# A four-layer convolution network on one core: the first function of each group of gelus or silus gets the lowest priority

## The chip, the cores and the metric

The kernel runs on one core of a Trainium2 chip. The metric is the device time of one execution in microseconds, the median of several runs. "ScalarE" is called ACT in the profile, "VectorE" DVE, "GpSimd" POOL, "TensorE" PE, and "SyncE", which issues most DMAs, SP.

## The reference, cut to what matters

Four layers follow each other on an input of 4 images of 64 x 64 tokens with 128 channels:

```python
x = _L0_conv_ref(x, ...)   # layernorm, projection, 3x3 depthwise conv, silu, selective scan in 4
                           # directions, layernorm, gate, projection, layernorm, MLP with gelu
x = _L1_conv_ref(x, ...)   # attention over all 4096 tokens
x = _L2_conv_ref(x, ...)   # 1x1 and 3x3 convolutions with hard_swish
x = _L3_conv_ref(x, ...)   # neighbourhood attention over 7 x 7, layernorm, MLP with gelu
```

The core of layer 0 is a recurrence over the 4096 tokens, for each of 256 channels and 16 states:

```python
def step(h, t):
    x_t, d_t, B_t, C_t = t
    h = jnp.exp(d_t[..., None] * A) * h + (d_t * x_t)[..., None] * B_t[:, :, None, :]
    return (h, jnp.einsum('bkdn,bkn->bkd', h, C_t))
```

## The kernel before, in words

The four images pass through the same stages. `scan_inputs` makes what the recurrence reads (delta, delta times x, B and C rows) and puts it into DRAM. `selective_scan` runs the recurrence of one image. `rest` does everything else for an image: `scan_output` (gate, projection and MLP of layer 0, and beside it, by turns, `layer3_mlp` of the image before), `layer1`, `layer2` and `layer3_attention`. `network` records scan(0), the scan inputs of the images 1 to 3, and then scan(i) followed by rest(i - 1). The last rest, of image 3, runs after the last scan with wider tiles.

In the scan a pair of 32 channels with 4 states fills 128 partitions, and time is cut into chunks of 512 steps. A unit of it is: GpSimd multiplies `du` by a B row (L501, 128 x 1024); ScalarE makes two "decays", exp(delta x A), of 128 x 512 each in PSUM (L507, three buffers); VectorE runs the recurrence over each (L509); the product with the C row is made by VectorE (L514) or, for 7 of 16 units (5 in image 0), by GpSimd (L522); ScalarE copies the last column as the state for the next chunk (L516 for one, L518 for two); TensorE sums over the states (L555). An image has 1024 decays, all four have 4096.

The exponential and the logarithm share one table set of ScalarE, which is the one that stays loaded. Gelu and silu need other sets. So they are done in groups: the class `Together` collects the functions of a group, lets all of them wait for the group's last matmul, and has the exponential's set loaded again behind them by `exp_table` (L96). There are 100 groups: 36 of up to four silus in `scan_inputs` (L359, L376), and 64 of four gelus in `mlp` (L226) and in the wide form of layer 3 (L1301). A group of gelus is then followed by the second product of its MLP (L233), which waits for it.

The order of each engine's instructions is fixed when the program is built. A scheduler goes through a simulated time and gives an engine, of the instructions that are ready, the one with the lowest priority number. Recorded code gets growing numbers from zero; `priority(tc, K, base)` gives what stands inside it numbers from `base` on. The scan has the base SCAN_FIRST = 10,000,000, so all else goes before it where both are ready. The groups have -100 x SCAN_FIRST: as soon as they are ready they go before everything. Which buffers are free is part of "ready".

Layernorm (L174 to L202) is mostly on ScalarE: two functions for the deviation, one for the sign (L192), four shifts (L194), four normalisations (L198), and one copy with scale and bias behind the transposition (L202).

Of the kernel before, what the change touches and what calls it, by code (L numbers as in the profile page):

```python
# [54 lines left out]
BEHIND = 2  # L55
ON_POOL = ((1, 4, 7, 10, 13), (0, 2, 4, 6, 9, 11, 13))
SCAN_FIRST = 10_000_000

# [16 lines left out]
@contextmanager  # L77
def priority(tc, K, base):

    kept = tc.cur_priority  # L80
    tc.cur_priority = K.next_priority.get(base, base)
    yield
    K.next_priority[base] = tc.cur_priority
    tc.cur_priority = kept


def after(tc, later, earlier, kind=mybir.DependencyClass.Sync):
    tc.add_manual_dep(
        later.ins, earlier.ins.name, mybir.DependencyInfo(kind, mybir.DependencyReason.DATA), reason="group"
    )  # L90


def exp_table(tc, K, done):

    with priority(tc, K, -100 * SCAN_FIRST):
        load = tc.nc.scalar.preload_act_table_set("natural_log_exp_and_others")  # L96
        after(tc, load, done, mybir.DependencyClass.NoSync)


class Together:  # L100
# [8 lines left out]
            after(self.tc, matmul, self.done)  # L109

    def run(self, last_matmul, acts):
        with priority(self.tc, self.K, -100 * SCAN_FIRST):
            for act in acts:
                self.done = act()
                after(self.tc, self.done, last_matmul)
        exp_table(self.tc, self.K, self.done)


# [146 lines left out]
def make_conv_diagonals(tc, K, A, out):  # L265
    nc = tc.nc
    with tc.tile_pool(name="mk_conv", bufs=1) as pool:
        convw = pool.tile([128, ND, 9], F32, name="convw")
        nc.sync.dma_start(convw, A["L0_conv_conv_w"])
        diag = pool.tile([128, ND, 9, 128], F32, name="conv_diag")  # L270
        for d in range(ND):
            for t in range(9):
                nc.scalar.activation(diag[:, d, t, :], K.ident, AF.Copy, scale=convw[:, d, t : t + 1])
        nc.sync.dma_start(out, diag)
# [1423 lines left out]
def network(tc, A, out):  # L1698
    nc = tc.nc
    with ExitStack() as ctx:  # L1700
# [26 lines left out]
        with ExitStack() as scan_ctx:  # L1727
            S = make_scan(scan_ctx, tc, K, A)
            make_conv_diagonals(tc, K, A, D.conv_diag)
            with priority(tc, K, SCAN_FIRST // 2):  # L1730
                with tc.tile_pool(name="mk_w2", bufs=1, side="right") as pool:
# [3 lines left out]
            for img in range(B):  # L1735
                with priority(tc, K, SCAN_FIRST):
                    selective_scan(tc, K, S, D, img)
# [94 lines left out]
```

## Time and profile before

| | |
|---|---|
| median of 3 runs | 8846.92 us (8845.23 to 8850.76) |
| the profiled execution | 8838.78 us, span 8837.0 us |
| busy: PE, DVE, ACT, POOL | 7047.0, 7137.4, 5686.9, 7046.7 us |
| decays (L507) | 4096, 690 ns each, 2781.9 us |
| B products (L501) | 2048, 2375 ns each, 4805.9 us |
| C products on GpSimd (L522) | 832, 2376 ns each, 1976.6 us |
| gelus (L226) | 224, 688 ns each, 135.5 us |
| loads of the gelu's table (L226) | 56, 1283 ns each, 71.8 us |
| loads of the exponential's table (L96) | 100, 1283 ns each, 128.3 us |

A row of a group in the profile gives line, engine, operation and tile, the count, the busy time, the mean of one and the idle time of its engine just before, with what ended it. A row of the timeline gives the start, the duration, and the idle time before it in square brackets. In a row of stretches of the span each engine's busy time stands with its count, then the granted clock of TensorE, the DMA engines' busy share and GB/s.

### The profile page before, as it was taken

How to read it: one execution, taken by the hardware profiler on the slowest of the kernel's cores; microseconds unless marked ns; L12 is line 12 of the kernel's file. 1: busy time of each engine (PE TensorE's matmuls, PEld its weight loads, DVE VectorE, ACT ScalarE, POOL GpSimd, SP SyncE). 2: the span in 40 equal slices, each digit the busy share in tenths (PEclk: the TensorE clock that was granted, in tenths of full speed). 3: DMA queues.
4: the chain of work that ended last, by engine and by line, in shares of the span. 5: the costliest groups of instructions: out<-in, count | busy, mean ns of one | idle time of the engine just before them, and what ended most of it. 6: DMA issues, size and time to landing. Idle time of an engine off the chain costs nothing. (4 is left out here: it accounts for less than half of the span.)

```text
span 8837.0 us, 102218 instructions
## 1 busy us (share of the span) xinstructions
PE 7047.0 (80%) x30532; PEld 2635.0 (30%) x30532; DVE 7137.4 (81%) x8531; ACT 5686.9 (64%) x11661; POOL 7046.7 (80%) x3079
## 2 busy tenths in 40 slices
PE   6745858687788898786788988877789887788988
PEld 2211313132332222333322223333322223344333
DVE  4788978787999999998899999998899999513433
ACT  5646767676676676666766676667766666454366
POOL 6888998989899999997799999998899989500000
PEclk8756869697799998898899998888899998899989
DMA  5777777777554556665455556575455565320020
GB/s 185 244 232 247 241 251 240 260 242 262 189 170 165 170 170 219 191 211 190 160 168 173 174 174 227 194 224 176 156 171 174 176 217 192 108 70 5 1 82 12
DMA packets 855474, 1572.03 MB, mean 178 GB/s; under 512 B 218341, under 2 KB 336764, under 8 KB 851197
## 3 DMA queue, kind: packets, MB, share of 16 engines
q1 hardware_dynamic: 724605, 1389.21, 48.1%
q10 hardware_dynamic: 130304, 176.19, 5.6%
q8 instruction: 245, 4.01, 0.2%
q14 instruction: 320, 2.62, 0.1%
HBM read 1273.92 MB, written 280.18 MB: 176 GB/s over the span
## 5 line engine op out<-in xcount | busy, mean ns | idle before, releaser
L501 POOL TENSOR_TENSOR dB<-du,b_rows 128x1024 f32<-128x1024 f32 x2048 | 4805.9, 2375 | 477.2 <-issue 124.7
L507 ACT ACTIVATE dA<-dt,w_A_log 128x512 f32<-128x512 f32 x4096 | 2781.9, 690 | 510.8 <-DVE hc L509 246.7
L509 DVE TENSOR_TENSOR_SCAN dA<-dA,state,dB 128x512 f32<-128x512 f32 x2128 | 2631.5, 1272 | 275.6 <-POOL dB L501 131.8
L522 POOL TENSOR_TENSOR hc<-hc,c_rows 128x1024 f32<-128x1024 f32 x832 | 1976.6, 2376 | 47.0 <-ACT state L518 21.7
L509 DVE TENSOR_TENSOR_SCAN hc<-dA,state,dB 128x512 f32<-128x512 f32 x1456 | 1801.1, 1267 | 180.5 <-ACT dA L507 105.8
L514 DVE TENSOR_TENSOR hc<-dA,c_rows 128x512 f32<-128x512 f32 x2432 | 1564.5, 675 | 74.4 <-PE py L555 59.3
L555 PE MATMUL py<-hc,pick 128*32 128x512 f32 x8192 | 1245.1, 683 | 392.0 <-POOL hc L522 299.8
L516 ACT COPY state<-dA 128x1 f32<-128x1 f32 x2128 | 326.9, 158 | 1271.7 <-DVE hc L514 1260.1
L845 PE MATMUL pa<-e,l_v 128*128 128x512 f32 x2048 | 1062.5, 651 | 20.3 <-ACT e L801 20.3
L797 PE MATMUL pair<-l_g,l_f 32*128 32x512 f32 x2048 | 532.8, 667 | 165.7 <-ACT e L801 119.1
L801 ACT ACTIVATE e<-pair 128x1024 f32<-128x1024 f32 (+1 forms) x448 | 508.4, 1135 | 231.4 <-PE pair L797 222.8
L985 POOL MEMSET l_h<- 64x128 f32 x8 | 1.6, 197 | 814.9 <-DVE l_h L959 814.9
L845 PEld LDWEIGHTS pa<-e,l_v 128*128 128x128 f32 x2048 | 374.3, 199 | 670.9 <-issue 615.1
L555 PEld LDWEIGHTS py<-hc,pick 128*32 128x32 f32 x8192 | 210.1, 116 | 1161.4 <-issue 471.1
L247 PE MATMUL ps<-band,w_conv_diag 128*128 128x504 f32 (+3 forms) x1152 | 500.4, 594 | 6.0 <-ACT delta L397 6.0
L1351 PE MATMUL pair<-table,ident 128*128 128x512 f32 x768 | 408.2, 657 | 98.7 <-ACT e L1361 76.2
L509 DVE TENSOR_TENSOR_SCAN dA<-dA,dB 128x512 f32<-128x512 f32 x304 | 356.1, 1212 | 66.3 <-POOL dB L501 52.5
L201 PE MATMUL ps<-ident,ln_xn 128*128 128x128 f32 x512 | 141.9, 371 | 325.2 <-ACT ln_xn L198 253.2
L328 POOL TENSOR_TENSOR du<-delta,xc 128x1024 f32<-128x1024 f32 x128 | 333.3, 2611 | 52.6 <-ACT delta L397 46.7
L1361 ACT ACTIVATE e<-pair 128x1024 f32<-128x1024 f32 (+1 forms) x224 | 254.8, 1137 | 178.6 <-PE pair L1355 177.8
L247 PEld LDWEIGHTS ps<-band,w_conv_diag 128*128 128x128 f32 x1152 | 221.3, 193 | 283.9 <-issue 263.8
L797 PEld LDWEIGHTS pair<-l_g,l_f 32*128 32x128 f32 x2048 | 140.6, 189 | 523.9 <-ACT e L801 264.4
(285 smaller groups left out, 8746.8 us busy)
## 6 DMA issues: line engine op xcount, KB each, us to landing
b_rows<-bc_dram SPq DMA_DIRECT2D x1024, 256.0 KB
c_rows<-bc_dram SPq DMA_DIRECT2D x1024, 256.0 KB
dt<-delta_dram SPq DMA_DIRECT2D x512, 512.0 KB
du<-du_dram SPq DMA_DIRECT2D x512, 512.0 KB
delta_dram<-delta ACTq DMA_DIRECT2D x128, 512.0 KB
du_dram<-du SPq DMA_DIRECT2D x128, 512.0 KB
table<-biasT_dram SPq DMA_DIRECT2D x72, 512.0 KB
y_first_dram<-y_sum ACTq DMA_DIRECT2D x128, 256.0 KB
```

Of the source, the lines that this page charges most:

```text
L247: mm = nc.tensor.matmul(out[:, r0 - row0 : r1 - row0, c0:c1], lhsT((dy + 1) * 3 + dx + 1), src[:, r0 + dy : r1 + dy, c0 + dx : c1 + dx], s ...
L328: nc.gpsimd.tensor_mul(du.rearrange("p d (a b) -> p d a b", b=H), deltas[b].rearrange("p d (a b) -> p d a b", b=H), tk,)
L501: nc.gpsimd.tensor_mul(dB, dus[pp], mid(bt, 2))
L507: nc.scalar.activation(dA, dts[pp][:, g, :], AF.Exp, scale=S.A[:, k, j, pr, g : g + 1])
L509: nc.vector.tensor_tensor_scan(hg[:, order], dA[:, order], dB[:, g, order], 0.0 if i == 0 else state[:, j, pr, g : g + 1], ALU.mult, ALU.add,)
L514: mm = nc.vector.tensor_mul(hc[:, g, :], dA, ct)
L522: made.append(nc.gpsimd.tensor_mul(hc, hc, mid(ct, 2)))
L555: mm = nc.tensor.matmul(py[0][32 * q : 32 * q + 32, :], S.pick, hcs[q // 2][:, q % 2, :], start=(k == 1 and j == 0), stop=(j == NJS - 1),)
L797: nc.tensor.matmul(ps[:, u, :], f[quad, t // 4, span(t % 4, 128)], g[quad, c, :], start=True, stop=True)
L801: made = nc.scalar.activation(e, ps, AF.Exp)
L845: nc.tensor.matmul(pa, v[:, 8 * q + t, :], es[q], start=(t == 0 and q == 0), stop=(t == 7 and q == 3),)
L1351: nc.tensor.matmul(ps[:, u, :], K.ident, t[:, u, :], start=True, stop=False)
```

## The change

In `Together.run` the first function of a group gets the base LAST x SCAN_FIRST = 500,000,000 in place of -100 x SCAN_FIRST, so that on its engine every other instruction that is ready goes before it. The others keep their number, and an order without a semaphore (NoSync) is added that puts them behind the first. The load of the exponential's set keeps its number and its place behind the last function.

```diff
 SCAN_FIRST = 10_000_000
+LAST = 50
...
     def run(self, last_matmul, acts):
-        with priority(self.tc, self.K, -100 * SCAN_FIRST):
-            for act in acts:
+        first = None
+        for act in acts:
+            with priority(self.tc, self.K, (LAST if first is None else -100) * SCAN_FIRST):
                 self.done = act()
                 after(self.tc, self.done, last_matmul)
+            if first is None:
+                first = self.done
+            else:
+                after(self.tc, self.done, first, mybir.DependencyClass.NoSync)
         exp_table(self.tc, self.K, self.done)
```

No computation is changed. What it changes is the built order of each engine's instructions. Behind the change, the line numbers of the kernel are 6 higher.

## The prediction

> **What bounds the kernel now.** I read the page first: VectorE (DVE) 81% and GpSimd (POOL) 80% busy, ScalarE (ACT) 64%, TensorE (PE) 80%. That is an average over stages, so I cut the span at the points where the sources of line change: scores of layer 1 (L801), attention products of layer 3 (L1384, L1390), scan_output (L618, L656). Busy time by stretch of the span, the stretch in front:
>
> ```profile
> core 0: us, PE busy (x) PEld busy (x) DVE busy (x) ACT busy (x) POOL busy (x), PEclk, DMA share, GB/s
> 4003.00:4453.00 450.00, 340.77 (x1378) 171.09 (x1378) 371.07 (x526) 325.02 (x736) 357.35 (x155) 0.83 0.53 172
> 4460.00:5130.00 670.00, 607.51 (x2472) 181.32 (x2470) 633.23 (x673) 445.61 (x844) 665.25 (x288) 0.94 0.53 172
> 5910.00:6358.00 448.00, 344.43 (x1379) 174.31 (x1379) 383.41 (x539) 327.62 (x724) 371.31 (x160) 0.83 0.55 179
> 6360.00:7030.00 670.00, 609.79 (x2505) 184.05 (x2502) 635.34 (x673) 452.21 (x876) 665.84 (x288) 0.95 0.52 172
> 7300.00:7600.00 300.00, 241.75 (x1397) 92.92 (x1390) 282.62 (x313) 194.50 (x417) 299.90 (x131) 0.86 0.58 192
> 7640.00:7770.00 130.00, 104.55 (x661) 44.64 (x660) 3.90 (x12) 33.41 (x45) 0.00 (x0) 0.93 0.14 42
> ```
>
> In layer 1 and layer 3 under a scan POOL is busy 99% and more: the scan runs at POOL's pace. In the two stretches that hold scan_output and the MLP of the image before (450 and 448 us, called A and B below) POOL is at 79% and 83%, and nothing is full: there engines wait for each other. The last row has no scan left at all, and layer 3 of image 2 still runs. VectorE's timeline at that place:
>
> ```profile
> 7636.64 1.27 DVE L514 TENSOR_TENSOR hc<-dA,c_rows 128x512 f32<-128x512 f32 x2
> 7672.43 0.69 DVE L1384 TENSOR_TENSOR oT<-rec,po 128x512 f32<-128x512 f32 x1 [34.52 <-ACT rec L1382]
> ...
> 7772.99 0.69 DVE L1390 TENSOR_TENSOR x<-x,pj 128x512 f32<-128x512 f32 x1 [2.17 <-PE pj L1388]
> 7776.04 0.27 DVE L600 MEMSET center<- 128x256 f32 x1 [2.36 <-DMA x_dram<-x]
> ```
>
> The last scan ends at 7638, layer 3 of image 2 at 7774, and only then does the final stage (L600, then 1061 us to the end) begin. The other hand-overs look alike: layer 3 of image 1 ends at 5896 and L618 of image 2 starts at 5910. So the end is set by the chain of rest() calls, one after the other, not by the scan alone.
>
> What ties the two: ACT's list is one fixed sequence in which rest's functions stand between decays (L507). Taking times of the 4096 decays from the trace, layer 1 passes 402 and 403 decays in 667.0 and 666.5 us, 1.657 us each, which is POOL's pace. A passes 210 decays in 445.0 us and B 216 in 441.7, so A is 97 us and B 84 us over that pace. Why, shows a gelu group on ACT (timeline) and then on DVE:
>
> ```profile
> 4094.01 0.14 ACT L516 COPY state<-dA 128x1 f32<-128x1 f32 x1
> 4094.16 1.28 ACT L226 ACT_TABLE_LOAD   x1
> 4095.46 2.42 ACT L226 ACTIVATE mlp_h<-ps,w_fc_b 128x512 f32<-128x512 f32 x4
> 4097.90 1.28 ACT L96 ACT_TABLE_LOAD   x1
> 4099.19 0.16 ACT L516 COPY state<-dA 128x1 f32<-128x1 f32 x1
> 4099.25 0.70 ACT L507 ACTIVATE dA<-dt,w_A_log 128x512 f32<-128x512 f32 x1
> ```
> ```profile
> 4094.48 1.27 DVE L514 TENSOR_TENSOR hc<-dA,c_rows 128x512 f32<-128x512 f32 x2
> 4099.98 1.29 DVE L509 TENSOR_TENSOR_SCAN dA<-dA,state,dB 128x512 f32<-128x512 f32 x1 [4.23 <-ACT dA L507]
> ```
>
> 5.02 us without a decay, and VectorE idles 4.23 us for one. Adding up VectorE's idle time from each group's start to 1.5 us after its end gives 52 us over the 16 groups of A and 48 over the 16 of B, 3.1 us a group.
>
> **What the Trainium skill says.** "ScalarE: Activation LUTs", section "What ACT_TABLE_LOAD costs", gives 1283 ns for a load plus some 1380 ns of drain. The trace agrees on 1283 (16 loads, mean 1283 ns) and not on the drain: the gelu starts 0.02 us after the load, and two loads and four gelus make 5.02 us. "TensorE: Matmul & The Clock Gate", section "Architectural detail", says that ACT's and DVE's queues are strictly first in, first out; the rows above agree, the ready decay stands behind the group. "Perfetto Trace Analysis", section "Optimization Strategy", asks to look for gaps inside the regime concerned; hence A and B alone.
>
> **The change part by part.** No instruction is added or removed, and the two loads per group stay, so direct work is 0. What moves is decided when the program is built, and I compared the two built orders.
>
> 1. Where it acts. ACT's order is the same up to position 6155 of 12239, which is 4036 us in the trace, and again from 7802 us on. The 36 silu groups and the first 8 gelu groups already stood behind the decays; the last 24 have no scan beside them. Only 32 gelu groups, those of A and B, move. Cost outside: 0, since those sequences are identical.
>
> 2. Decays before the group. Counting decays minus state copies ahead of each group gives the decays ready in the three PSUM buffers: 2.75 on average in A before and 2.9 after, 2.4 and 2.3 in B. So they mostly stood there already; what now moves ahead of gelus is as much layernorm work (L194, L198) as decays.
>
> 3. Length of the stretches without a decay. I add ACT's work between each two decays from the rows' means (load 1.283, gelu 0.605, L198 0.42, L194 0.21, state 0.15 to 0.19 us) and take what exceeds 3.9 us, two decays' work of VectorE (twice 1.27 for L509 and 0.675 for L514). A: 46.8 us before, 37.1 after. B: 36.6 before, 39.0 after. Price: A and B differ by 13.2 us over the pace and by 10.2 in this sum, 1.3 us for each. So A gains 9.7 x 1.3 = 12.6 us and B loses 2.4 x 1.3 = 3.1: together -9.5 us. From below: all groups as long as now, 0; from above: all VectorE idle time in the groups gone, -100.
>
> 4. The lead of rest over the scan. Counting decays that stand before the same step of rest: the first score function of layer 1 has 2271 before it in both orders for image 1, and 3347 before, 3333 after for image 2. The lead shrinks to 3 at the start of layer 3 and is 16 again at L1381 of the fifth chunk, 4077 against 4061. Those 16 decays no longer stand between rest and its end; at the trace's 1.65 us each (204 decays from number 3857 to 4061 took 337.1 us) it is -26.5 us. Afterwards 16 more decays run beside the last three chunks: the sixth took 68.7 us partly under the scan, a full one takes some 79, so I give 3 us back. Can rest go that fast? Image 1's first chunks of layer 3 held 46, 45 and 45 decays and took 74.2, 73.7 and 72.2 us; later ones held 50, 49 and 51 and took 86.1, 82.9 and 85.7. Image 2 goes from 48 a chunk to 45, a rate already seen.
>
> 5. Other queues. DVE, PE and SP follow the same plan; POOL's list differs in 59 of 3083 places. SP's loads of x (L612, L1330) move up by as much as 14 places, among transfers that use half the DMA engines' time; I cost them at nothing, one missed landing would be some 2.4 us, as the L188 wait for x in A.
>
> Sum: -9.5 - 26.5 + 3 = -33 us. Against the profiled execution (8838.78, span 8837.0, 1.8 around it) that is 8806; it lies 8 us under the median, so for the median I say 8846.9 - 33 = 8814.
>
> **The rivals.** (a) TensorE paces layer 3, not the decays: PE is 80% busy there with and without scan, and its busy time counts waits badly. Then the lead is worth nothing, as the products (L555) it passes only come later, and -9.5 us remain: 8837. The 45-decay chunks speak against it. (b) The gelus become late. A group that waits for one more layernorm block waits 4 x 0.21 + 4 x 0.42 = 2.5 us; the 16 groups of scan_output lie on rest's chain (the other 16, of the image before, have slack): +40 us, 8887. It decides if the fc2 products behind the gelu, not the shared list, set when a chunk ends; the gain of 33 is lost from 2.1 us a group on. For it: gelus now follow L194 and L198 blocks in several groups. Against: rest's steps stand at equal or smaller decay counts at the end of A and B. (c) Stalls fall further: seven of the first eight gelu groups, which have always stood behind a decay, leave VectorE idle 1.8 us each. If all 32 come down to that, 32 x 1.3 = -42, with the lead -65: 8782. Against: step 2.
>
> **How the numbers follow.** Forecast 0.58, (a) 0.20, (b) 0.10, (c) 0.12. Some 0.2% (18 us) is what a measurement of this kernel can tell from no change. Of the forecast 0.52 lies beyond it; with (c) and a little of (a), faster 0.67; the rest of (a) and of the forecast, same 0.22; (b), slower 0.11. The range 8782 to 8853 ends at (c) below and takes in all of (a) above; beyond it lie (b) and part of (c). The forecast's own range is 8795 to 8830.
>
> **What would show it.** Right: A shorter by some 12 us with POOL above 80% in it; B with 10 decays fewer; layer 3 of image 2 ends near 7741 instead of 7774, and some 115 us instead of 136 after the last scan. Step 3 is wrong if A is as long as before; step 4 if five chunks of layer 3 take as long with 45 decays each as with 48. Wrong altogether: gelus that hold up L233, seen as PE idle time released by mlp_h growing, or a final stage of other than 1061 us.

## The result, and the profile after

The changed kernel takes 8832.41 us (median; 8822.39 to 8842.44), the kernel before, run beside it, 8849.52 us. The ratio is 0.9981, 95% interval 0.9975 to 0.9987: 17 us faster (12 to 22), where 33 were forecast. Its profiled execution took 8831.36 us, 7.4 less than that of before; but up to decay 2061, where both run the same order, it had already lost 7.7 us (its B products took 2388 ns each up to there, against 2370). From there to the end it is 15.1 us shorter, which agrees with the medians.

The same stretches as before the change, cut at the same sources of line (busy time by stretch of the span, kernel after):

```profile
core 0: us, PE busy (x) PEld busy (x) DVE busy (x) ACT busy (x) POOL busy (x), PEclk, DMA share, GB/s
4011.00:4451.00 440.00, 342.48 (x1372) 169.85 (x1373) 370.76 (x526) 324.56 (x736) 356.93 (x155) 0.84 0.55 176
5908.00:6346.00 438.00, 336.35 (x1375) 162.42 (x1373) 370.79 (x525) 320.69 (x706) 352.03 (x152) 0.85 0.54 175
6350.00:7020.00 670.00, 605.60 (x2447) 181.40 (x2446) 635.39 (x675) 449.14 (x872) 666.82 (x289) 0.94 0.52 172
7300.00:7600.00 300.00, 245.62 (x1416) 94.14 (x1408) 280.63 (x312) 194.94 (x418) 299.71 (x131) 0.86 0.60 193
7650.00:7760.00 110.00, 87.78 (x528) 37.75 (x528) 3.91 (x12) 27.20 (x38) 0.00 (x0) 0.89 0.15 50
```

A (first row) holds the same 526 VectorE and 155 GpSimd instructions as before, in some 10 us less. B (second row) is shorter too, but with 152 GpSimd instructions in place of 160: 206 decays fall into it, not 216. In layer 3 of image 2 (fourth row) TensorE does 1416 products in 300 us where it did 1397, with no more VectorE work: rest goes faster there, and fewer decays stand in its way (counted below). The last row, without a scan, is what the change shortened most. VectorE's timeline at the scan's end, kernel after:

```profile
7646.01 1.27 DVE L520 TENSOR_TENSOR hc<-dA,c_rows 128x512 f32<-128x512 f32 x2
...
7764.20 0.69 DVE L1396 TENSOR_TENSOR x<-x,pj 128x512 f32<-128x512 f32 x1 [1.51 <-PE pj L1394]
7767.25 0.27 DVE L606 MEMSET center<- 128x256 f32 x1 [2.36 <-DMA x_dram<-x]
```

From the last scan product to the final stage it was 7637 to 7776; now it is 7646 to 7767. A gelu group of A on ACT, kernel after:

```profile
4093.80 0.69 ACT L513 ACTIVATE dA<-dt,w_A_log 128x512 f32<-128x512 f32 x1 [1.10 <-DVE hc L515]
4094.51 1.28 ACT L232 ACT_TABLE_LOAD   x1
4095.80 2.42 ACT L232 ACTIVATE mlp_h<-ps,w_fc_b 128x512 f32<-128x512 f32 x4
4098.24 1.28 ACT L97 ACT_TABLE_LOAD   x1
```

The group itself has not changed: 5.02 us without a decay. Nor have the stalls beside the groups: VectorE idles 51.1 us around the 16 groups of A (52.2 before) and 52.5 around those of B (47.8 before). What the change says it does, decays ahead of gelus, is not where its gain comes from: VectorE's idle time in A as a whole fell from 79 to 69 us (first row of each table), so the stalls that shrank lie between the groups.

A table of the kernels on which the argument rests shows where it does come from. I take the time between numbered decays, since each decay is the same work in every order. "To 3111" is from decay 2271, "to 4096" from 3347; "tail" is from the start of decay 4096 to the end of layer 3 of image 2. All in us, from the profiled executions; the lead is the number of decays ahead of the division by the attention sums (L1381) in the fifth chunk of image 2's layer 3. The experiments e1 to e13 are described in the next section; "not held" means that two small VectorE instructions no longer wait for GpSimd. e5 and e7 move work ahead of decay 2061 too.

| kernel | lead | A: 2061-2271 | to 3111 | hand-over: 3111-3131 | B: 3131-3347 | to 4096 | tail | sum | final stage |
|---|---|---|---|---|---|---|---|---|---|
| before | 4077 | 445.0 | 1423.2 | 40.5 | 441.7 | 1275.8 | 139.9 | 3766.1 | 1063.3 |
| after | 4061 | 435.6 | 1424.5 | 49.1 | 445.2 | 1273.6 | 121.7 | 3749.7 | 1064.7 |
| e1, first group of A | 4061 | 434.6 | 1428.1 | 45.2 | 442.3 | 1270.2 | 121.9 | 3742.3 | 1061.7 |
| e2, one group of B | 4096 | 447.2 | 1423.2 | 40.3 | 436.0 | 1269.8 | 169.7 | 3786.2 | 1055.3 |
| e5, MLP joins later | 4063 | 421.5 | 1424.3 | 41.7 | 442.2 | 1272.7 | 121.7 | 3724.1 | 1069.6 |
| e6, fewest stalls | 4093 | 424.5 | 1424.0 | 31.4 | 439.0 | 1272.9 | 157.9 | 3749.7 | 1048.6 |
| e7, both | 4063 | 432.3 | 1417.9 | 32.8 | 437.2 | 1281.4 | 118.7 | 3720.3 | 1064.7 |
| e11, before, not held | 4077 | 447.2 | 1424.0 | 38.3 | 443.8 | 1276.0 | 139.8 | 3769.1 | 1057.2 |
| e12, after, not held | 4061 | 435.0 | 1428.5 | 44.1 | 446.1 | 1269.7 | 121.7 | 3745.2 | 1066.2 |
| e13, e1, not held | 4061 | 435.8 | 1421.6 | 46.4 | 444.3 | 1269.7 | 121.7 | 3739.6 | 1062.4 |

Between before and after the scan's second half took 1.8 us *longer* (-9.4 in A, +8.6 at the hand-over to B, +3.5 in B, -0.9 elsewhere), and the tail is 18.2 us shorter. So by the scan's clock the whole gain stands behind the last decay.

Rest's own steps give a second clock, and on it the gain stands in other places (`y` is the first function of `scan_output`, L622; all in us):

| stretch of rest | before | after |
|---|---|---|
| A: first `y` to the first score of layer 1 | 444.0 | 434.4 |
| layers 1 to 3 of image 1 | 1443.1 | 1436.7 |
| hand-over: end of layer 3 to the first `y` of B | 20.6 | 26.1 |
| B: first `y` to the first score | 441.7 | 432.0 |
| image 2: first score to the first L1381 | 921.3 | 937.1 |
| first to fifth L1381 | 319.8 | 301.5 |
| fifth L1381 to the end of layer 3 | 174.0 | 180.0 |

Rest gains 9.6 us in A, 9.7 in B, which has 10 decays fewer in it, and 18.3 in the first chunks of layer 3, with 180 decays in place of 192. What it gained in B it loses again in layers 1 and 2, where its lead falls from 14 decays to 4. The pairs e8 and e9, e11 and e12, e3 and e4, whose orders differ in the same way, show the gain between the first and the fifth L1381 too: 20.4, 20.7 and 18.8 us.

The final stage is the same but for two small instructions (and for e3 and e4, which are not in the table) and still lies between 1049 and 1070 us; a single profile tells no difference of under some 10 us there, which is why I compare stretches and medians, not spans.

### The profile page after: what moved, and what is told of

It reads as the page before. It is cut to its first block, busy times and chain, and to the rows that moved or that the text cites. A ratio compares the mean times of both kernels' runs of the same rounds, so it can differ in the third digit from the quotient of the medians.

```text
span 8829.6 us, 102177 instructions
## 1 busy us (share of the span) xinstructions
PE 7045.8 (80%) x30532; PEld 2620.1 (30%) x30532; DVE 7143.3 (81%) x8531; ACT 5689.1 (64%) x11661; POOL 7049.6 (80%) x3079
## 5 line engine op out<-in xcount | busy, mean ns | idle before, releaser
L528 POOL TENSOR_TENSOR hc<-hc,c_rows 128x1024 f32<-128x1024 f32 x832 | 2000.5, 2404 | 55.8 <-ACT state L524 27.1
```

Of the source, the lines that this page charges most:

```text
L528: made.append(nc.gpsimd.tensor_mul(hc, hc, mid(ct, 2)))
```

## The experiments

Theory 1 is the forecast's: ACT's one fixed list couples two chains, and the time follows from the lead (decays that stand between rest and its end) and from the stalls between decays. Theory 2: the groups themselves gain, each by the decays put ahead of it. Theory 3 is rival (a): the lead is worth nothing, stalls alone count.

**e1: one group late, the first of A.** `Together.run` counts its calls from zero; number 44 is the first group of A. Built one at a time, 28 of the 32 groups of A and B leave ACT's order as it was. ACT's order then differs from the changed kernel's in 126 of 12239 places.

```diff
+        K = self.K
+        K.calls = getattr(K, 'calls', -1) + 1
+        late = K.calls == 44
...
-            with priority(self.tc, self.K, (LAST if first is None else -100) * SCAN_FIRST):
+            with priority(self.tc, self.K, (LAST if first is None and late else -100) * SCAN_FIRST):
```

> Only one of the 100 groups gets the low priority: the first gelu group of stretch A (image 0's layer 3 MLP, first chunk). The built order is then that of the changed kernel but for 126 of ScalarE's 12239 places. Theory 1 (the change is one decision of the planner that tips the whole order; the time follows stretches without a decay and rest's lead over the scan): the same gain as the whole change, -17 us (-10 to -25). Theory 2 (each group that lets decays go first saves its own stall): one of 32, -0.5 us. Theory 3 (TensorE paces layer 3, a lead is worth nothing): -10 us, the stalls of A alone.

8827.93 us, ratio 0.9981 (0.9972 to 0.9990): -17 us, the gain of the whole change. One group of 100 is enough; theory 2 falls.

**e2: one group late, in B** (the same edit with number 64).

> Again one group alone, in B (the fifth one). A keeps the order of before; behind B rest lags the scan: 4096 decays before L1381 of the fifth chunk of image 2's layer 3, in place of 4077 before and 4061 with the change. Stretches without a decay in B fall from 36.6 to 32.5 us over the bound. Theory 1: 19 decays of lag cost 19 x 1.3 to 1.65 = 25 to 31 us, the stalls give 5 back: slower by 20 to 26 us. Theory 2: -0.5 us. Theory 3: -5 us.

8862.58 us, ratio 1.0019 (1.0012 to 1.0025): 17 us slower. The sign turns with the lead, as theory 1 says (19 decays more ahead of the same step, and the tail is 29.8 us longer), while B itself is 5.7 us shorter. Theory 3 has the wrong sign. The size is below the 20 to 26 expected. That sum took nothing back for the last three chunks, which took 168.9 us in place of 174.0, since fewer decays ran beside them.

**e3 and e4: no load of the gelu's set.** The gelus are computed as exponentials, so that their set isn't loaded (64 loads less); the output is not the network's. e3 is the kernel before, e4 the changed one.

```diff
-            lambda f=f: nc.scalar.activation(hT[:, f, :], phs[f], AF.Gelu, bias=P.b1[:, f : f + 1])
+            lambda f=f: nc.scalar.activation(hT[:, f, :], phs[f], AF.Exp, bias=P.b1[:, f : f + 1])
```

> The kernel before with exp in place of gelu, so that the 64 loads of gelu's table fall away (the output is that of another function; the loads of the exponential's set stay). Every engine's order is that of before, but for these loads. It prices a stretch without decays: the sum over 3.9 us falls by 20.1 us in A and 19.7 in B. Theory 1 with 1.3 us each: A and B shorter by 26 us each, image 0's eight groups some 10, the final stage 24 x 1.28 = 31: together -93 us. If a load in A or B costs only its own time on ScalarE: 16 x 1.28 = 20 each. If the stalls of A and B are hidden and another engine sets rest's pace: the final stage's -31 alone.

> The same replacement in the changed kernel; every engine's order is that of the changed kernel but for the 64 loads. Against the run without loads in the order of before: the sums over 3.9 us are 9.8 us less in A and 2.2 more in B, the lead is 16 decays again. Theory 1: again some 17 us faster than that run (10 to 25), -110 us in all. Theory 2 (the change helps by hiding the loads behind ready decays): about half as much, since half of the group's overhead is gone: 8 us. Theory 3: 10 us.

e3: 8785.31 us, ratio 0.9922 (0.9908 to 0.9935), -69. e4: 8762.79 us, 0.9897 (0.9882 to 0.9912), -91. The change is still worth some 22 us, with an uncertainty nearly as large by the two intervals, where each group's stretch is 1.28 us shorter. Stretch by stretch it is there as well (A 8.1 us shorter, tail 20.9 shorter, hand-over 8.1 longer), so it doesn't live on the loads. The -110 expected of e4 is missed along with e3's -93. A group of e3 on ACT (timeline):

```profile
4101.91 0.69 ACT L507 ACTIVATE dA<-dt,w_A_log 128x512 f32<-128x512 f32 x1
4102.53 2.40 ACT L226 ACTIVATE mlp_h<-ps,w_fc_b 128x512 f32<-128x512 f32 x4
4104.95 1.28 ACT L96 ACT_TABLE_LOAD   x1
```

Sixteen loads of 1.283 us make 20.5 us; decays 2061 to 2271 took 424.5 us, 20.5 less than before, and those of B 23.1 less. That is the price of a stall which the prediction needed: 1.0 to 1.1 us for each microsecond without a decay, not 1.3. e3 misses its expectation of 93 for that reason, and because the final stage, where no decays wait, gave back little: 9 us less in the profile, where 31 were expected and single profiles scatter by some 10.

**e5, e6, e7: another order by other means.** The groups keep their priority. In e5 the MLP of layer 3 takes its turns in `scan_output` only once fewer than six chunks are left to begin; in e6 it has no turn between layernorm and MLP; e7 has both, with five chunks.

```diff
-            if before is not None:
+            if before is not None and len(todo) < NCH - 2:
                 step(before)
...
         layernorm_T(tc, K, pool, psum, x, n_w, n_b, xnT)
-        yield
```

> The kernel before, groups as they were; the MLP of layer 3 of the image before joins the turns of scan_output only when fewer than six chunks are left to begin. Nothing is left out. ACT's built order has 16.5 us less above 3.9 us between decays in A and 1.7 less in B, and 4063 decays instead of 4077 ahead of L1381 of the fifth chunk. Theory 1 (lead and stalls set the time, however the order comes about): stalls 16.5 + 1.7 at 1.0 each, lead 14 x 1.65 = 23, some 9 given back in layer 3 and the hand-over: -32, between -22 and -38, clearly below the changed kernel's -17. Rival (only the priority of the groups works; a later start of the MLP merely shifts its work to the end of A and B, where it stands on rest's chain): 0 to +15.

> The kernel before without the turn between layernorm and MLP of layer 3 (the yield in layer3_mlp). Nothing is left out. Of the built orders this has few long stretches without a decay: 11.7 us less above 3.9 us in A, 7.8 less in B. But 4093 decays stand ahead of L1381 of the fifth chunk, 16 more than before. Theory 1: stalls -19.5, lead +26, giveback of the other sign -6, hand-over 0 to -4: about 0, between -8 and +8; A shorter by 12 us, B by 0 to 8, and more than 165 us of layer 3 of image 2 behind the last decay in place of 140. Rival (the stalls between decays alone set the time, the lead is worth nothing, as TensorE paces layer 3): -19.

> Both edits together on the kernel before: the MLP of layer 3 joins when fewer than five chunks are left, and has no turn between layernorm and MLP. Nothing is left out. 15.1 us less above 3.9 us in A and 7.7 less in B, and 4063 decays ahead of L1381 of the fifth chunk. Theory 1: stalls -23, lead -23, 9 given back: -37, between -27 and -45, the shortest of all without a load taken out. Rival (stalls alone): -23. Rival (lead alone): -14 to -23, as the changed kernel.

e5: 8807.72 us, ratio 0.9964 (0.9951 to 0.9978), -32, as theory 1 said. e6: 8828.05 us, 0.9987 (0.9980 to 0.9994), -11, a miss for theory 1, which allowed -8 to +8, and for the rival's -19. e7: 8796.39 us, 0.9950 (0.9937 to 0.9964), -44, the shortest of the three, and it beats both the kernel before and the changed one. Busy time by stretch of e6, A and then the tail:

```profile
core 0: us, PE busy (x) PEld busy (x) DVE busy (x) ACT busy (x) POOL busy (x), PEclk, DMA share, GB/s
4016.40:4439.10 422.70, 323.44 (x1376) 160.47 (x1379) 366.55 (x517) 320.37 (x729) 350.20 (x151) 0.87 0.54 178
7610.00:7755.00 145.00, 114.08 (x672) 48.90 (x668) 5.55 (x21) 37.93 (x58) 0.00 (x0) 0.90 0.12 39
```

A is 21 us shorter than before, but 145 us and more of layer 3 stand alone at the end. By the table e6's scan is 34.4 us shorter and its tail 18.0 longer, where e5's scan is only 23.8 shorter and its tail 18.2 shorter: e6's scan shrank more than e5's, and still its sum is 25.6 us longer. So the lead is real. Its worth, "to 4096" and tail together against before, is 20.4 us for 16 decays in the changed kernel, 15.1 for 16 in e6, 23.8 for 19 in e2, 21.3 for 14 in e5 and 15.6 for 14 in e7: 0.9 to 1.5 us a decay, less than the 1.65 that a decay takes. e6's miss is a stall term that was too small (34 instead of 19.5), 9.1 of it at the hand-over, which I had left out again.

**e8 to e14: what ate the gain at the hand-over to B.** The hand-over is the largest loss in the table, +8.6 us. The timeline of GpSimd and VectorE there, kernel before, then after:

```profile
5901.60 5.60 DVE L601 TENSOR_TENSOR center<-center,ident 128x128 f32<-128x128 f32 x1
...
5902.37 4.68 POOL L501 TENSOR_TENSOR dB<-du,b_rows 128x1024 f32<-128x1024 f32 x2
...
5909.71 2.43 POOL L501 TENSOR_TENSOR dB<-du,b_rows 128x1024 f32<-128x1024 f32 x1 [2.66 <-DVE hc L509]
```
```profile
5894.68 8.92 DVE L607 TENSOR_TENSOR center<-center,ident 128x128 f32<-128x128 f32 x1
...
5900.99 2.47 POOL L528 TENSOR_TENSOR hc<-hc,c_rows 128x1024 f32<-128x1024 f32 x1
...
5903.53 2.45 DVE L515 TENSOR_TENSOR_SCAN dA<-dA,state,dB 128x512 f32<-128x512 f32 x2
```

One addition of 128 x 128 lasts 5.60 us before and 8.92 after. In both it ends some 0.15 us behind the end of a run of GpSimd instructions (5907.05 and 5903.46); in the final stage, where GpSimd is idle, it lasts 0.29 us. "SBUF — State Buffer" of the Trainium skill, section "Who interferes with whom", says that a VectorE instruction with two SBUF inputs contends with a GpSimd instruction that reads SBUF; the trace agrees, and shows it waiting for a whole run of them. e8 (kernel before), e9 (after) and e10 (e7) give it one input:

```diff
-        nc.vector.tensor_add(center[:, 0, :], center[:, 0, :], K.ident)
+        nc.vector.tensor_scalar_add(center[:, 0, :], K.ident, -1.0 / DI)
```

> The kernel before with L601 reading one SBUF tensor (ident plus a constant) in place of two. Nothing is left out; ACT's built order is unchanged. In the trace of before L601 lasts 11.22, 0.59 and 5.60 us at the hand-overs to scan_output, each time up to the end of a run of GpSimd instructions, and 0.29 us where no scan runs. Theory 1 (VectorE is held up while GpSimd works from SBUF, and the scan behind it): L601 0.2 to 0.3 us everywhere; GpSimd's idle time of 2.5 us behind it in the first case and some 5 us in the third is saved: -7, between -3 and -12. Rival (bystander: the hand-over waits for something else, the layer 3 end or the loads): 0, between -2 and +2.

> The same line in the changed kernel, where L607 lasts 8.92 us at the hand-over to B and decays 3111 to 3131 take 49.1 us against 40.5 before. Nothing is left out. Theory 1 (the longer wait of that one instruction is what ate part of the gain there): decays 3111 to 3131 come down to some 35 to 40 us in both kernels, and this one gains 8 us more than it: -17 - 10 = -27 against before, between -22 and -33. Rival (bystander): -17.

> The same line in the kernel whose MLP of layer 3 joins later and has no turn, where L601 lasts 11.2, 6.76 and 4.16 us. Nothing is left out. Theory 1: the earlier -44 and 7 more, -51, between -45 and -58. Rival (bystander): -44.

Ratios 1.0000 (0.9992 to 1.0008), 0.9981 (0.9973 to 0.9989) and 0.9944 (0.9930 to 0.9957). The first two are what the rival expected, the third (-50) lies in theory 1's range; but none of them tests either, since the wait stayed, as VectorE's timeline of e8 shows:

```profile
5909.30 5.68 DVE L601 TENSOR_SCALAR center<-ident 128x128 f32<-128x128 f32 x1
```

The same section says that a scalar operation from SBUF to SBUF can contend as well, under conditions, and that a reduction never does on trn2. e11 (before), e12 (after), e13 (e1) and e14 (e7) make both L601 and L598 by reductions; the product with `onorm_b` is left out in all four.

```diff
-            nc.vector.tensor_scalar_mul(out_proj_b[:, d, :], out_proj[:, d, :], onorm_b[:, d : d + 1])
+            nc.vector.tensor_reduce(out_proj_b[:, d, :], out_proj[:, d, :].rearrange("p (j t) -> p j t", t=1), AX.X, ALU.add)
...
-        nc.vector.tensor_add(center[:, 0, :], center[:, 0, :], K.ident)
+        nc.vector.tensor_reduce(center[:, 0, :], K.identc.rearrange("p t j -> p j t"), AX.X, ALU.add)
```

> The kernel before, with L601 and L598 made by reductions: center is the sum over the identity and a constant row beside it, and out_proj_b is a copy of out_proj (its product with onorm_b is left out). ACT's order stays the same but for 171 of 12239 places, with the same decay counts ahead of every step. With a single-input addition L601 still lasted 11.15 and 5.68 us; the Trainium skill, SBUF - State Buffer, section Who interferes with whom, says of trn2 that a reduction never contends with GpSimd. Theory 1 (VectorE held beside GpSimd, and the scan behind it, is a cost of its own): L601 and L598 last under 0.5 us everywhere, decays 3111 to 3131 fall from 40.5 us to 33 to 36, and the time by 7, between -3 and -12. Rival (bystander: what VectorE loses there, another wait takes): L601 short, decays 3111 to 3131 about 40, time 0, between -2 and +2.

> The same two lines in the changed kernel (the product with onorm_b is left out here too). Theory 1: decays 3111 to 3131 fall from 49.1 us to 35 to 40 and the time against the kernel before is -27, between -22 and -33. Rival (bystander): decays 3111 to 3131 about 47, time -17 as the changed kernel.

> The kernel in which only the first group of A is late (8827.93, -19.5 as the changed kernel), with the two lines made by reductions; the product with onorm_b is left out. Theory 1 (VectorE held beside GpSimd at the hand-over to B is what ate about 10 us of the change): -38 against before, between -32 and -44, as the changed kernel without the hold. Rival (the reductions give every order the same 11 us, and the 38 of the one kernel was scatter over its 5 runs): -28, between -24 and -32. Decays 3111 to 3131 fall from 45.2 us to 40 to 44 under both.

> The kernel whose MLP of layer 3 joins later and has no turn, with the two lines made by reductions; the product with onorm_b is left out. There L601 lasted 11.2, 6.76 and 4.16 us and decays 3111 to 3131 take 32.8 us, their pace under a full GpSimd. Theory 1: at its hand-over to B there is nothing left to save, so only the first two hand-overs gain: -44 to -49 as it is, and 5 to 8 more, -52. Rival (the reductions give every order 11): -58; rival (they give the orders with the lead 20): -67.

Now the wait is gone; VectorE and ACT of e12 at the hand-over (timelines of one engine each):

```profile
5892.93 0.42 DVE L609 TENSOR_REDUCE center<-ident 128x128 f32<-128x256 f32 x1
5893.27 2.46 DVE L517 TENSOR_TENSOR_SCAN dA<-dA,state,dB 128x512 f32<-128x512 f32 x2
```
```profile
5909.89 0.30 ACT L182 ACTIVATE ln_rstd<-ln_mv,eps 128x4 f32<-128x4 f32 x1 [2.78 <-DVE ln_mv L198]
...
5912.90 0.85 ACT L202 ACTIVATE ln_shift<-ln_mv,ln_less 128x1 f32<-128x1 f32 x4 [1.90 <-DMA x<-x_dram]
```

e11: 8838.76 us, ratio 0.9988 (0.9982 to 0.9995), -11. e12: 8811.65 us, 0.9953 (0.9940 to 0.9967), -42. e13: 8816.22 us, 0.9965 (0.9952 to 0.9979), -31. e14: 8799.72 us, 0.9943 (0.9930 to 0.9957), -50, as e10. So the two held-up instructions did cost the kernel before some 11 us (4 to 16 by the interval). In its profile 5.4 us of that show at the first hand-over (decays 1040 to 1072 take 77.7 us in place of 83.1) and 2.2 at the one to B. e14 came out as theory 1 said, e13 as the rival said (-28), and e12 gained more than theory 1's range of -22 to -33 allows. e11 to e14 change L598 as well as L601, so the two lines aren't told apart.

By the decays the hold is not what made the loss at the hand-over to B: decays 3111 to 3131 took 44.1 us in e12 and 46.4 in e13, not the 35 to 40 and 40 to 44 expected, against 38.3 in e11, so most of the 8.6 us is still there without it. By rest's own steps it is open: from the end of layer 3 to the first `y` of B it took 20.6 us before, 26.1 after and 22.4 in e1; without the hold it took 18.8 in e11, 19.0 in e12, where no loss is left, and 21.6 in e13.

Counted decay by decay, decay 3122 waits 15.35 us after the one before it in the changed kernel and 6.57 in e12; but decay 3128 waits 7.83 and then 12.03. In e1 and e13 the pair is 11.66 and 7.94, then 7.02 and 13.65. Much of a wait that was taken away returned six decays later. The first hand-over does the same: decay 1050 waits 13.9 us before and 4.7 in e11, decay 1056 6.6 and then 10.2. What stands ahead of decay 3128 shows ACT's timeline, kernel before and then after:

```profile
5916.26 0.68 ACT L507 ACTIVATE dA<-dt,w_A_log 128x512 f32<-128x512 f32 x1
5916.88 1.06 ACT L622 ACTIVATE y<-ps 128x512 f32<-128x512 f32 x2
...
5919.79 0.69 ACT L507 ACTIVATE dA<-dt,w_A_log 128x512 f32<-128x512 f32 x1
```
```profile
5914.22 1.06 ACT L628 ACTIVATE y<-ps 128x512 f32<-128x512 f32 x2
5917.54 0.30 ACT L180 ACTIVATE ln_rstd<-ln_mv,eps 128x4 f32<-128x4 f32 x1 [2.26 <-DVE ln_mv L196]
...
5919.72 1.63 ACT L204 ACTIVATE ln_xn<-x,ln_shift,ln_rstd 128x128 f32<-128x128 f32 x4
...
5921.43 1.91 ACT L513 ACTIVATE dA<-dt,w_A_log 128x512 f32<-128x512 f32 x3
```

Before, decays 3128 to 3131 stand ahead of the first functions of B, and 3132 to 3135 between these and its single layernorm functions. After, the whole layernorm of the first block is ahead of decay 3128, and ACT waits in it for VectorE's statistics of an x that has just been loaded. The decays stand in line behind a stage that starts. This is read from the trace; that the row of functions is the cause was not tried by moving it alone. e5 and e7 have the same lead as the changed kernel with 41.7 and 32.8 us there, so the loss is no necessary price of the lead.

What stays open: e12 and e13 lie 20 to 31 us under e11, the change against before 17. By their intervals this may be one number. The first hand-over doesn't explain it: without the hold it gained 5.4 us in e11, 6.4 in e12 and 6.0 in e13, against before, after and e1.

## Why the prediction was right or wrong

The forecast (8814) was too low by 18 us. The measured time lies inside the wide range, just above the forecast's own (8795 to 8830), and near rival (a)'s 8837, though not for that rival's reason. The mechanism was right in kind, and the sum lacked a cost. By the steps, profile against profile:

**Step 1** (only the groups of A and B move): right for the built order, and e1 shows more: the first of them tips the rest. Its "cost outside: 0" can't be told from scatter: the 7.7 us lost ahead of the change and the 1.4 in the final stage stand where both orders are the same.

**Step 2** (decays ahead of groups hardly change): right; VectorE's idle time around the groups is 103.6 us after and 100.0 before. With it rival (c) falls.

**Step 3** (the stalls): A forecast at -12.6, measured -9.4, as the price is 1.0, not 1.3 (e3). I had got 1.3 by dividing two differences between A and B, which differ in more than stalls. B forecast +3.1, measured +3.5.

**Step 4** (the lead): right, and nearly so in size. From decay 3347 to L1381 of the fifth chunk the kernel took 1241.7 us before and 1215.3 after, 26.4 less, where 26.5 were forecast. The test that the prediction named for this step, chunks with 45 decays against 48, came out for it: four chunks took 301.5 us in place of 319.8. But the part given back is 6.0 us, not 3: the last three chunks, beside which more decays run, took 180.0 us in place of 174.0. Together -20.4, against -23.5. e2 and e6 confirm it from the other side. Rival (a) falls with them.

**Step 5** is the step that failed most: "I cost them at nothing". It is the only step that touches what waits at the start of a stage, and no term of the sum stood for the hand-over to B, which lost 8.6 us by the decays (5.5 by rest's own steps). The same pairs of orders show the loss again: 48.3 us against 40.2 in e4 and e3, 46.8 against 40.1 in e9 and e8. I had cut the stretches of step 3 at the first `y` of B, so the start of the stage, where loads, statistics and layernorm follow each other with nothing to cover them, was in no stretch. The order counts gave a hint: 13 decays instead of 10 between the last L1381 of layer 3 and B. What the moved order waits for there is read from the trace only; its cause stays open.

**Final stage**: +1.4, within what one program varies by.

The sum is -9.4 + 1.3 (between A and the hand-over) + 8.6 + 3.5 - 20.4 + 1.4 = -15.0 (each rounded), against -33; of the 18 missing, 8.6 are the hand-over, 3.2 the price of a stall, 3.1 the lead with what it gives back, and the rest is small. The signs named under "What would show it" came: A shorter by 9.6 with GpSimd at 81%, B with 10 decays fewer, and 118 us instead of 136 from the last scan product to the end of layer 3, where 115 were named. Layer 3 of image 2 ended at 7765, not near 7741, since 7.7 us were lost ahead of the change and the rest is the sum above. Rival (b), late gelus, doesn't show: the idle time of TensorE that a gelu ended ahead of the MLP's second product fell from 32.9 to 26.6 us.

## What to carry to other kernels

Where two pipelines share an engine's fixed list, count for each order what stands ahead of the *end* of the chain that finishes last, and price it by the time between equally numbered steps of the other chain, less what the later steps give back; set the steps of both chains side by side, since a gain may stand in different places on the two clocks; a change of priority may act through one instruction that tips the order, so try it alone, and try other ways to the same order. Cut the stages so that every hand-over belongs to one of the counted stretches. When a wait is taken away, look a few steps on in the same list: here much of it came back six decays later.

## What the runs showed of the hardware that was not expected

A 128 x 128 VectorE operation from SBUF to SBUF waited as long as GpSimd ran without a break: 11.22 us in the first hand-over, 8.92 and 5.60 in others, 0.29 beside an idle GpSimd; with one input it was held as well (11.15 and 5.68 us), as a reduction not at all (0.42). A table load cost little beyond its 1.283 us: sixteen fewer, 20.5 us, shortened A by 20.5 us and B by 23.1. Between profiles the same GpSimd product (128 x 1024) had means from 2366 to 2424 ns, and nearly the same final stage took 1049 to 1070 us.
